# Queries of tiles 1 to 7 read from a second, transposed copy of the input and normalised on GpSimd in place of normalised rows transposed on TensorE

## The chip, the cores and the metric

The program runs on one core of one Trainium2 chip. Its engines are TensorE (PE, matmuls and transposes; its weight loads are shown apart as PEld), VectorE (DVE), ScalarE (ACT), GpSimd (POOL) and SyncE (SP, which here only issues transfers). Each engine takes its instructions in order; between engines there are semaphores. A transfer (DMA) is put on a queue by the engine that issues it, and an engine that has to wait before it issues one holds back everything behind it on that engine. The metric is device time in microseconds, the median of several executions; the profile is one further execution.

## The reference, cut to what matters

One layer in float32: cross-attention whose queries are the normalised input, then a gated MLP with a top-k selection, then a mixture of small experts. The change touches the first line alone.

```
def _layernorm(x, axis=-1, eps=1e-05):
    m = jnp.mean(x, axis=axis, keepdims=True)
    v = jnp.var(x, axis=axis, keepdims=True)
    return (x - m) / jnp.sqrt(v + eps)

def _L0_xattn_ref(q, k, v, start_pos, mask):       # 32 heads of 32, 8 key/value heads, 4 query heads each
    scores = jnp.einsum('bsgrd,btgd->bgrst', xq, xk) / math.sqrt(HEAD_DIM) + mask
    probs = jax.nn.softmax(scores, axis=-1)
    out = jnp.einsum('bgrst,btgd->bsgrd', probs, xv)

x = x + _L0_xattn_ref(_layernorm(x), ctx_1024, ctx_1024, 0, mask)   # x: 16 x 64 x 1024, ctx: 16 x 1601 x 256
x = x + _L0_attn_ref(_layernorm(x), w_gate, w_up, w_down)           # width 2752
x = x + _L0_ffn_ref(_layernorm(x), router_w, router_b, A, Bm)
```

## The kernel before, in words

The 16 x 64 = 1024 rows of x are cut into 8 tiles of 128 rows (NT = 8); tile i holds the batches 2i and 2i + 1. The first half of the program is the attention, the second the MLP and the experts, which a planner orders by costs; the change lies wholly in the first half, whose order on every engine is the order in which the Python program emits it (the helper `InOrder`, line 87, keeps it; as it emits every operation, all these instructions carry line 95 in the profile, so they are told apart by the names of their tiles).

The attention runs over 64 groups (lines 238 to 360): a group is one batch b, one half h of the 8 key/value heads, and one pair rh of the four query heads that share a key head. So a tile has 8 groups; in the loop at line 419, n is the group, m = n % 8 its place in the tile, and i = n // 8 + 1 is the *next* tile, whose queries are made ready in this one. Each turn of the loop has two halves, d = 0 and 1, and each half is one round of software pipelining:

- PE computes one half of the scores of the *next* group (`scores`, eight matmuls `ps` or `shared` <- kT, qt), then the value products of the *last* group (`values`, `shared` <- pT, v), then transposes the exponentials of two heads of *this* group (`turn`, 26 transposes `pt` <- ident, sc).
- DVE adds the mask and takes the maximum (`masked`, `sc` <- ps, mask), ACT takes the exponentials (`sc` <- sc, nm), and both copy the transposed blocks out of PSUM (`pT` <- pt).

The queries of tile i come about inside the turns of the tile before it. At m = 2 SP issues the load of x[i] (line 424). DVE takes the statistics of its two column halves at (m, d) = (4, 0) and (5, 0) (`Norm.half`). At (5, 1) DVE ends them, POOL raises the variance to the power -1/2 (`rstd_q`) and scales the rows (`scaled_rows`, `xn` <- x, mv_q, rstd_q, two instructions). At (6, 1) and (7, 1) `turn_queries` makes PE transpose four 128 x 128 blocks for each head half h (`ptq` <- ident, xn), and ACT copies them from PSUM to `qt` and multiplies by 1/sqrt(32). The scores of the first group of tile i, which read half h = 0 of `qt`, are emitted at (7, 0) of the turns before it, and half h = 1 is first read at m = 1 of its own turns. Tile 0 has its own path ahead of the loop.

Around this there are two streams of transfers. On SP's queue, `load_kv(b + 1)` (line 191) is emitted within `scores(0)` of the group (b, h = 0, rh = 1), that is at (m, d) = (4, 0) and (0, 0). It issues two key tiles (`kT`) and two value tiles (`v`, each in two transfers, 12 blocks and a tail of 65 rows). The pools `kT` and `v` have three buffers each, and a batch takes two of each, so the second key tile waits until the scores of (b, 0, 1) are done, and the second value tile until the *value products* of (b, 0, 1) are done: these are emitted two turns later, at m = 6 or m = 2, d = 1. On SP follow the x load at m = 2 and, at m = 4 before the keys, the store `xs` of a finished tile.

On POOL, `sums_in`, `sums_made` and `sums_out` (lines 166 to 180) prepare weight sums for the MLP, one unit a turn: a load of some 700 KB, four subtractions, a store. POOL also normalises and adds the attention's output (`finish_tile`, at (1, 1) and (2, 0): `att` <- att, rs and `x` <- x, att). The tile `att` and the tile `xn` take turns in one buffer (`xnp`, one buffer, tag xn).

```
        for d in range(2):
            ...
                following.scores(d)
            ...
                groups[n - 1].values(d)
            ...
            if i < NT and d == 1 and m >= 6:
                turn_queries(i, xn, m - 6)
            ...
            copies = group.turn((2 * d, 2 * d + 1))
            ...
                if (m, d) == (5, 1):
                    norm.end()
                    xn = scaled_rows(i, norm, pool)
```

Of the kernel before, what the change touches and what calls it, by code (L numbers as in the profile page):

```python
# [9 lines left out]
F32 = mybir.dt.float32  # L10
# [6 lines left out]
ALU = mybir.AluOpType  # L17
# [3 lines left out]
P = 128  # L21
B, S, D = 16, 64, 1024
T, C = 1601, 256
HD = 32
NT = B * S // P
# [26 lines left out]
EPS = 1e-5  # L52
# [4 lines left out]
def tile_perceiver_layer(  # L57
    ctx: ExitStack,
    tc: tile.TileContext,
    x_in: bass.AP,  # L60
    ctx_v: bass.AP,
    ctx_t: bass.AP,
    mask: bass.AP,
# [11 lines left out]
    dram = ctx.enter_context(  # L75
        tc.tile_pool(name="dram", bufs=1, space=bass.MemoryType.DRAM)
    )
    small = ctx.enter_context(tc.tile_pool(name="small", bufs=4))
# [3 lines left out]
    neg_half = const.tile([P, 1], F32, name="neg_half")  # L82
    nc.gpsimd.memset(neg_half, -0.5)

    x = {}

    class InOrder:


        def __init__(self, engine):  # L90
            self.engine = engine
# [7 lines left out]
    pe, dve, act = InOrder(nc.tensor), InOrder(nc.vector), InOrder(nc.scalar)  # L99
    pool, sp_queue = InOrder(nc.gpsimd), InOrder(nc.sync)  # L100

    class Norm:


        def __init__(self, xt, name):
            self.xt, self.name = xt, name
            self.st = small.tile([P, 2, 6], F32, tag="st", name=f"st_{name}")

        def half(self, j):
# [2 lines left out]
        def end(self):  # L112
            name = self.name
            mv = small.tile([P, 2], F32, tag="mv", name=f"mv_{name}")
            dve.bn_aggr(mv, self.st)
            ve = small.tile([P, 1], F32, tag="ve", name=f"ve_{name}")
            dve.tensor_scalar(ve, mv[:, 1:2], EPS, None, ALU.add)
            rstd = small.tile([P, 1], F32, tag="rstd", name=f"rstd_{name}")
            pool.tensor_tensor(rstd, ve, neg_half, ALU.pow)
            self.mean, self.rstd = mv[:, 0:1], rstd  # L120

# [5 lines left out]
    def new_pool(stack, name, bufs, side="left", space=bass.MemoryType.SB):  # L129
        return stack.enter_context(  # L130
            tc.tile_pool(name=name, bufs=bufs, side=side, space=space, reuse_waits="tile")
        )
# [3 lines left out]
    a1 = new_pool(early, "a1", 1)  # L136
    ktp = new_pool(early, "kT", 3)
    qtp = new_pool(early, "qT", 2)
    scp = new_pool(early, "sc", 2)
    xnp = new_pool(late, "xn", 1, "right")  # L140
# [30 lines left out]
    def sums_made(u):  # L171
        b11, b12, b21, b22 = (sums[u][:, j, :] for j in range(4))
        pool.tensor_tensor(b12, b12, b11, ALU.subtract)
        pool.tensor_tensor(b22, b22, b12, ALU.subtract)
        pool.tensor_tensor(b11, b22, b11, ALU.subtract)
        pool.tensor_tensor(b21, b21, b22, ALU.subtract)

    def sums_out(u):
        (_, t), _ = sum_columns(u)
        pool.dma_start(t, sums[u])  # L180

    def load_x(i, parts=1):
        x[i] = xp.tile([P, D], F32, tag="x", name=f"x{i}")
        for j in range(parts):
            cols = slice(j * D // parts, (j + 1) * D // parts)
            sp_queue.dma_start(x[i][:, cols], x_in[i * P : (i + 1) * P, cols])

    mask2 = a1.tile([P, T], F32, name="mask2")
    qT, kv, oT, rs_tok = {}, {}, {}, {}
# [25 lines left out]
    def scaled_rows(i, norm, engine):  # L215

        xn = xnp.tile([P, 2, 4, 4, HD], F32, tag="xn", name=f"xn{i}")
        xv = x[i].rearrange("p (h g r d) -> p h r g d", h=2, g=4, r=4)
        for h in range(2):
            engine.tensor_scalar(  # L220
                xn[:, h], xv[:, h], norm.mean, norm.rstd, ALU.subtract, ALU.mult
            )
        return xn

    def turn_queries(i, xn, h):

        if h == 0:
            qT[i] = qtp.tile([P, 2, 2, 4, S], F32, tag="qt", name=f"qt{i}")
        pt = ps_t.tile([P, 4, P], F32, tag="pt", name=f"ptq{i}_{h}")
        for r in range(4):  # L230
            pe.transpose(pt[:, r, :], xn[:, h, r].rearrange("p g d -> p (g d)"), ident)
        act.activation(
            qT[i][:, h].rearrange("p b r s -> p r b s"),
            pt.rearrange("p r (b s) -> p r b s", b=2),
            AF.Copy, scale=1.0 / math.sqrt(HD),
        )
# [127 lines left out]
    def finish_tile(i, h, home=ps_t, tag="pt"):  # L364


        if h == 0:
            att[i] = xnp.tile([P, 2, 4, 4, HD], F32, tag="xn", name=f"att{i}")
        rows = att[i][:, h]
        pt = home.tile([P, 4, P], F32, tag=tag, name=f"pto{i}_{h}")  # L370
        for r in range(4):
            pe.transpose(
                pt[:, r, :], oT[i][:, h, r].rearrange("p b s -> p (b s)"), ident
            )

        def add():
            pool.tensor_tensor(
                rows, rows, rs_tok[i][:, h].unsqueeze(3).to_broadcast([P, 4, 4, HD]),
                ALU.mult,
            )  # L380
            xv = x[i].rearrange("p (h g r d) -> p h r g d", h=2, g=4, r=4)
            pool.tensor_tensor(xv[:, h], xv[:, h], rows, ALU.add)

        return (rows, pt.rearrange("p r (g d) -> p r g d", g=4)), add
# [12 lines left out]
    norm = Norm(x[0], "q0")  # L397
# [3 lines left out]
    xn = scaled_rows(0, norm, dve)  # L401
# [17 lines left out]
    for n in range(ng):  # L419
        i, m = n // 8 + 1, n % 8  # L420
        group = groups[n]
        last = n == ng - 1
        if m == 2 and i < NT:
            load_x(i)
        if m == 4 and n > 8:
            sp_queue.dma_start(xs[i - 2], x[i - 2])
        if n == ng - 3:
            for j in range(2):
                x[j] = xp.tile([P, D], F32, tag="x", name=f"x{j}_f")
                sp_queue.dma_start(x[j], xs[j])  # L430
        for d in range(2):
            add = None
            following = groups[n + 1] if not last else None
            if following:
                following.scores(d)
            if n > 0:
                groups[n - 1].values(d)
            if following:
                following.masked(d)
            on_act = [0, 1, 2] if last else [0, 1, 2, 3, 5]  # L440
            if i < NT and d == 1 and m >= 6:
                turn_queries(i, xn, m - 6)
            if n > 8 and 3 <= 2 * m + d <= 4:
                copy, add = finish_tile(i - 2, 1 - d)
                act.copy(*copy)
            copies = group.turn((2 * d, 2 * d + 1))
            for j, copy in enumerate(copies):
                if j in on_act:
                    act.copy(*copy)
                else:  # L450
                    dve.tensor_copy(*copy)
            if n > 0:
                groups[n - 1].keep(d)
                if d == 1:
                    groups[n - 1].inverse()
            for g in range(2):
                if d == 0:
                    group.softmax(2 + g)
                elif following:
                    following.softmax(g)  # L460
            if add:
                add()
            if i < NT:
                if (m, d) == (4, 0):
                    norm = Norm(x[i], f"q{i}")
                if (m, d) in ((4, 0), (5, 0)):
                    norm.half(m - 4)
                if (m, d) == (5, 1):
                    norm.end()
                    xn = scaled_rows(i, norm, pool)  # L470
            if d == 1 and 0 <= n - 3 < 3 * NU:
                sums_made(n - 3)
                sums_out(n - 3)
            if d == 1 and 0 <= n - 2 < 3 * NU:
                sums_in(n - 2)
            if last:
                xn = first[d].tile([P, D], F32, tag=("xn", "oT")[d], name=f"xn_f{d}")
                norm = Norm(x[d], f"f{d}")
                norm.half(0)
                norm.half(1)  # L480
                norm.end()
                dve.tensor_scalar(xn, x[d], norm.mean, norm.rstd, ALU.subtract, ALU.mult)
                first_xn[d] = xn
# [49 lines left out]
    s, hS, held_h, hs, a, marked = {}, {}, {}, {}, {}, {0: [], 1: []}  # L533
# [716 lines left out]
    over = add("PE", 1.1, end, [t] + hs[0], rank["g0"] - 5)  # L1250
# [36 lines left out]
class Plan:  # L1287
# [20 lines left out]
    def add(self, engine, cost, emit, deps, rank, takes=None, frees=None, margin=0.0):  # L1308
        holds, frees = (
            [hold for hold in (h if isinstance(h, tuple) else (h,)) if hold]  # L1310
            for h in (takes, frees)
        )
        task = self.Task(engine, cost, emit, deps, rank, holds, margin)
        for hold in frees:
            hold.freed_by = task
        self.tasks.append(task)
        return task
# [98 lines left out]
```

## Time and profile before

| | |
|---|---|
| median of 3 executions | 1696.45 us (1695.98 to 1696.63) |
| the profiled execution | 1695.55 us, of which its span (first to last instruction) is 1693.7 us |
| busy share of the span | PE 98%, DVE 85%, ACT 75%, POOL 33% |
| attention | from the start to about 818 us |
| granted TensorE clock, mean | 0.996 of full speed |
| transfers | 384.53 MB, mean 227 GB/s |

In lists of instructions the fields are: start, time taken, engine, line, operation, the tile written <- the tiles read, shapes, count; an idle time in square brackets is what the engine waited before it and for whom. In groups and tiles, three numbers with strokes are the shortest, the middle and the longest duration in ns. In lists of transfers the last number is the middle time in us from the issue to the landing.

### The profile page before, as it was taken

How to read it: one execution, taken by the hardware profiler on the slowest of the kernel's cores; microseconds unless marked ns; L12 is line 12 of the kernel's file. 1: busy time of each engine (PE TensorE's matmuls, PEld its weight loads, DVE VectorE, ACT ScalarE, POOL GpSimd, SP SyncE). 2: the span in 40 equal slices, each digit the busy share in tenths (PEclk: the TensorE clock that was granted, in tenths of full speed). 3: DMA queues.
4: the chain of work that ended last, by engine and by line, in shares of the span. 5: the costliest groups of instructions: out<-in, count | busy, mean ns of one | idle time of the engine just before them, and what ended most of it. 6: DMA issues, size and time to landing. Idle time of an engine off the chain costs nothing. (4 is left out here: it accounts for less than half of the span.)

```text
span 1693.7 us, 38371 instructions
## 1 busy us (share of the span) xinstructions
PE 1666.9 (98%) x15098; PEld 1190.4 (70%) x15098; DVE 1437.5 (85%) x3654; ACT 1262.8 (75%) x1716; POOL 560.1 (33%) x584
## 2 busy tenths in 40 slices
PE   8999999999999999999899999999989999999998
PEld 6888888888888888888666666645645646645644
DVE  7998989899898988988429999999999999999603
ACT  6999999999999999999246675677467772778010
POOL 2045455455545544110121212222381023430631
PEclk9999999999999999999999999999989999999999
DMA  8245656565564655131799999988959979888973
GB/s 252 92 131 185 209 165 213 180 220 167 196 216 153 221 192 190 41 97 61 275 293 330 306 291 307 290 277 274 345 175 302 307 248 320 273 297 270 324 262 135
DMA packets 132018, 384.53 MB, mean 227 GB/s; under 512 B 9440, under 2 KB 60928, under 8 KB 131840
## 3 DMA queue, kind: packets, MB, share of 16 engines
q1 hardware_dynamic: 112976, 312.83, 56.2%
q0 software_dynamic: 18432, 68.16, 11.6%
q8 instruction: 120, 1.97, 0.5%
q10 hardware_dynamic: 432, 1.09, 0.2%
q14 instruction: 58, 0.48, 0.1%
HBM read 339.58 MB, written 42.47 MB: 226 GB/s over the span
## 5 line engine op out<-in xcount | busy, mean ns | idle before, releaser
L95 DVE CUSTOM_DVE_ANT_0 sc<-ps,mask 128x512 f32<-128x512 f32 (+2 forms) x896 | 468.3, 587 | 30.4 <-PE ps L95 29.1
L95 ACT ACTIVATE sign<-a,cand 128x2752 int8<-128x2752 f32 x136 | 351.8, 2587 | 111.0 <-DVE cand L95 111.0
L95 ACT ACTIVATE sc<-sc,nm 128x1601 f32<-128x1601 f32 x256 | 415.7, 1629 | 9.3 <-DVE nm L95 9.3
L95 PE MATMUL pt<-ident,sc 128*128 128x128 f32 (+1 forms) x3328 | 390.5, 274 | 1.9 <-ACT sc L95 1.7
L95 DVE TENSOR_SCALAR_CACHE_REDUCE junk<-a,cand 128x2752 uint8<-128x2752 f32 x124 | 381.7, 3078 | 4.0
L95 PEld LDWEIGHTS pt<-ident,sc 128*128 128x128 f32 (+1 forms) x3328 | 362.0, 141 | 22.9 <-issue 19.0
L95 ACT COPY pT<-pt 128x512 f32<-128x512 f32 x636 | 335.5, 599 | 23.4 <-PE pt L95 11.9
L95 POOL TENSOR_TENSOR tw<-tw 128x344 f32<-128x344 f32 (+1 forms) x192 | 176.0, 927 | 275.9 <-DMA tw<-in_wg_dram 93.0
L95 PE MATMUL pg_g<-w_g,hS 128*128 128x344 f32 x896 | 262.9, 455 | 2.8 <-DMA w_g<-ts 2.1
L95 PE MATMUL pg_u<-w_u,hS 128*128 128x344 f32 x896 | 263.4, 452 | 0.0
L95 PEld LDWEIGHTS pg_g<-w_g,hS 128*128 128x128 f32 x896 | 170.6, 191 | 91.8 <-issue 4.9
L95 PE MATMUL pd<-w_d,s 128*128 128x512 f32 x528 | 233.9, 597 | 0.0
L95 PEld LDWEIGHTS pg_u<-w_u,hS 128*128 128x128 f32 x896 | 169.0, 190 | 87.2 <-issue 3.1
L95 PE MATMUL shared<-pT,v 128*32 128x128 f32 x6656 | 208.1, 274 | 3.6 <-DVE oT L95 3.6
L95 PE MATMUL ps<-kT,qt 32*128 32x512 f32 (+2 forms) x1792 | 210.9, 538 | 0.3 <-DVE mx L95 0.3
L95 PEld LDWEIGHTS shared<-pT,v 128*32 128x32 f32 x6656 | 174.1, 110 | 52.1 <-issue 45.1
L95 PEld LDWEIGHTS pd<-w_d,s 128*128 128x128 f32 x528 | 99.3, 192 | 114.8 <-issue 113.4
L95 DVE COPY pT<-pt 128x512 f32<-128x512 f32 (+1 forms) x260 | 139.9, 558 | 45.2 <-PE pt L95 45.2
L95 PEld LDWEIGHTS ps<-kT,qt 32*128 32x128 f32 x1792 | 97.7, 184 | 52.8 <-DVE pT L95 27.5
L95 ACT ACTIVATE s<-s 128x344 f32<-128x344 f32 (+1 forms) x70 | 36.5, 535 | 75.8 <-DVE s L95 75.7
L95 POOL TENSOR_TENSOR s<-s,rank 128x688 f32<-128x688 f32 x32 | 62.4, 1963 | 77.5 <-DVE rank L95 76.9
L95 DVE DVE_READ_ACCUMULATOR2_ANT mx<- 128x1 f32 x1024 | 84.3, 82 | 0.0
(326 smaller groups left out, 1411.7 us busy)
## 6 DMA issues: line engine op xcount, KB each, us to landing
w_g<-ts SPq DMA_DIRECT2D x64, 688.0 KB, 4.2
w_u<-ts SPq DMA_DIRECT2D x64, 688.0 KB, 4.2
w_d<-ts SPq DMA_DIRECT2D x48, 768.0 KB, 4.2
w_g<-in_wg_dram SPq DMA_DIRECT2D x48, 688.0 KB, 4.1
w_u<-in_wu_dram SPq DMA_DIRECT2D x48, 688.0 KB, 4.8
w_d<-in_wd_dram SPq DMA_DIRECT2D x36, 768.0 KB, 5.1
kT<-in_ctx_t_dram SPq DMA_DIRECT2D x31, 800.5 KB, 6.7
v<-in_ctx_v_dram SPq DMA_DIRECT2D x32, 768.0 KB, 5.3
```

What stands on the lines that cost most here:

```text
L95: return tc.keep_in_program_order(getattr(self.engine, op)(*args, **kwargs))
```

## The change

A second copy of x, `x_q`, is laid out on the host: for each tile 128 partitions (four key heads by 32 head dimensions) by 1024 columns (h, batch, r, row). A tile of it is what the transposes made, without the normalisation. As mean and 1/std belong to the columns of that copy, they have to lie along the free axis and on every partition: they are written to device memory (256 floats) and read back to all partitions (`row`, 128 x 256). POOL then subtracts and multiplies, four instructions of 128 x 512. The factor 1/sqrt(32) goes into the variance, which is multiplied by 32 before the power.

In order: at (4, 0) the statistics begin and SP is given the load of `xq`, into the buffer of `xn`; at (4, 1) they end, POOL takes the power, and SP is given the store of `stats` and the load of `row`; at (5, 1) POOL is given the four instructions that write `qt`. The transposes at (6, 1) and (7, 1) and ACT's copies of them are gone. `load_kv` of (4, 0) is emitted ahead of all three new transfers, as it is part of `scores(0)`.

```
         def end(self):
...
-            dve.tensor_scalar(ve, mv[:, 1:2], EPS, None, ALU.add)
-            rstd = small.tile([P, 1], F32, tag="rstd", name=f"rstd_{name}")
-            pool.tensor_tensor(rstd, ve, neg_half, ALU.pow)
-            self.mean, self.rstd = mv[:, 0:1], rstd
+            dve.tensor_scalar(ve, mv[:, 1:2], EPS, self.over, ALU.add, ALU.mult)
+            pool.tensor_tensor(mv[:, 1:2], ve, neg_half, ALU.pow)
+            self.mean, self.rstd, self.both = mv[:, 0:1], mv[:, 1:2], mv
...
+    def row_tile(i):
+        row = a1.tile([P, 2, P // S, S], F32, tag="row", name=f"row{i}")
+        stats = dram.tile([1, 2 * P], F32, tag=f"stats{i}", name=f"stats{i}")
+        sp_queue.dma_start(
+            stats.rearrange("o (k p) -> (o p) k", k=2), norm.both
+        )
+        sp_queue.dma_start(
+            row.rearrange("p k b s -> p (k b s)"), stats.to_broadcast([P, 2 * P])
+        )
+        return row
+
+    def load_queries(i):
+        raw = xnp.tile([P, 2, 4, 4, HD], F32, tag="xn", name=f"xq{i}")
+        raw = raw.rearrange("p h r g d -> p (h r g d)")
+        sp_queue.dma_start(raw, x_q[i])
+        return raw.rearrange("p (h b r s) -> p h b r s", h=2, b=P // S, r=4)
+
+    def scale_queries(i, raw, row):
+        qT[i] = qtp.tile([P, 2, 2, 4, S], F32, tag="qt", name=f"qt{i}")
+        mean, rstd = (
+            row[:, k].unsqueeze(2).to_broadcast([P, P // S, 4, S]) for k in range(2)
+        )
+        for h in range(2):
+            pool.tensor_tensor(raw[:, h], raw[:, h], mean, ALU.subtract)
+            pool.tensor_tensor(qT[i][:, h], raw[:, h], rstd, ALU.mult)
...
-            if i < NT and d == 1 and m >= 6:
-                turn_queries(i, xn, m - 6)
...
                 if (m, d) == (4, 0):
-                    norm = Norm(x[i], f"q{i}")
-                if (m, d) in ((4, 0), (5, 0)):
-                    norm.half(m - 4)
+                    norm, raw = Norm(x[i], f"q{i}", float(HD)), load_queries(i)
+                if m == 4:
+                    norm.half(d)
+                if (m, d) == (4, 1):
+                    norm.end()
+                    row = row_tile(i)
                 if (m, d) == (5, 1):
-                    norm.end()
-                    xn = scaled_rows(i, norm, pool)
+                    scale_queries(i, raw, row)
```

More of the change, by code (lines that the diff above doesn't have):

```diff
@@ L60, in tile_perceiver_layer @@
     x_in: bass.AP,
+    x_q: bass.AP,
     ctx_v: bass.AP,
@@ L102, in tile_perceiver_layer, with __init__ @@
     class Norm:
-        def __init__(self, xt, name):
-            self.xt, self.name = xt, name
+        def __init__(self, xt, name, over=1.0):
+            self.xt, self.name, self.over = xt, name, over
             self.st = small.tile([P, 2, 6], F32, tag="st", name=f"st_{name}")
@@ L1389, in wide @@
         return w.transpose(3, 0, 5, 1, 4, 2).reshape(4, P, GW)
+    x_q = np.asarray(x).reshape(NT, P // S, S, 2, 4, 4, HD)
+    x_q = x_q.transpose(0, 4, 6, 3, 1, 5, 2).reshape(NT, P, D)
     laid_out = {
         "x": np.asarray(x).reshape(B * S, D),
+        "x_q": x_q,
         "ctx_v": ctx_v,
```

## The prediction

> **What bounds the kernel now.** I read the page's engine shares first, then the order of PE around the place where the queries are used, then SP's own waits, then POOL, and last the landing times of transfers. The first lines are the page's shares and its slices for PE.
>
> ```profile
> PE 1666.9 (98%) x15098; PEld 1190.4 (70%) x15098; DVE 1437.5 (85%) x3654; ACT 1262.8 (75%) x1716; POOL 560.1 (33%) x584
> ...
> PE   8999999999999999999899999999989999999998
> ```
>
> In the attention (the left half) PE has no idle slice: whatever makes PE wait there lengthens the run one for one, and whatever PE loses shortens it. The timeline of PE at the end of tile 2's turns, where tile 3's queries are due, shows where each half ends:
>
> ```profile
> 294.60 1.38 PE L95 MATMUL ps<-kT,qt 32*128 32x512 f32 x11
> ...
> 296.16 1.74 PE L95 MATMUL shared<-pT,v 128*32 128x128 f32 x56
> 297.83 0.66 PE L95 MATMUL ptq<-ident,xn 128*128 128x128 f32 x4
> 298.32 3.00 PE L95 MATMUL pt<-ident,sc 128*128 128x128 f32 x26
> 301.25 1.38 PE L95 MATMUL ps<-kT,qt 32*128 32x512 f32 x11
> ```
>
> The first four lines are (m, d) = (6, 1): scores, value products to 297.9, the query transposes of h = 0, the 26 transposes. At 301.25 the half (7, 0) begins with the first scores of tile 3; they are the first to read the new `qt`. The next half has no slack before it: there is no bracket with an idle time.
>
> SP's waits in total, SP's timeline over the same stretch, and one later place on SP:
>
> ```profile
> SPq L95 <- PE shared L95: 642.0, 44, 24.1
> ```
>
> ```profile
> 297.96 1.16 SPq L95 DMA_DIRECT2D v<-in_ctx_v_dram  x2
> 299.16 0.36 SPq L95 DMA_DIRECT2D kT<-in_ctx_t_dram  x1
> ```
>
> ```profile
> 747.44 0.35 SPq L95 DMA_DIRECT2D xs<-x  x1
> 747.88 5.56 SPq L95 DMA_DIRECT2D x_f<-xs  x2
> ```
>
> This decides the case. SP stands for 642 us behind the value products: the second `v` load of a batch needs the buffer that they free. The one emitted at (4, 0) is released at 297.96, right after the products of (6, 1). What is emitted behind it in SP's order (here the next batch's kT) starts at 299.16, 1.20 us later. In the other six tiles the pair stands the same way (v at 99.14, 198.54, 397.37, 496.78, 596.19, 695.60, each 3.3 us ahead of the scores that open the next tile). Landing times:
>
> ```profile
> v<-in_ctx_v_dram SPq DMA_DIRECT2D x32, 768.0 KB, 5.3
> ...
> out_dram<-s SPq DMA_DIRECT2D x16, 256.0 KB, 2.4
> x<-in_x_dram SPq DMA_DIRECT2D x7, 512.0 KB, 5.8
> ...
> x_f<-xs SPq DMA_DIRECT2D x2, 512.0 KB, 3.2
> ```
>
> **What goes.** For each of 7 tiles, 8 query transposes: `ptq` starts at 297.83 and the next work at 298.32, so 0.49 us of PE for a half h, 0.98 us a tile, 6.9 us in all. They lie on the bound, so the gain is real. Also gone: ACT's 14 copies to `qt` at 0.60 us (8.4 us), and POOL's 14 `xn` instructions at 2.07 us (29 us). Both engines keep up with PE here (PE waited for ACT's `sc` 1.7 us in the whole run), so these count nothing.
>
> **What moves.** `xq`, `stats` and `row` are issued by SP, in program order. `load_kv` of (4, 0) is emitted ahead of them within `scores(0)`, so all three stand behind the second `v` load, and that waits until the value products of (6, 1) end. They are emitted at (4, 0) and (4, 1), about 30 us ahead of use, but can start only at the place of the 299.16 line. The first scores of the next tile come, with the `ptq` of (6, 1) gone, 301.25 - 0.49 - 297.96 = 2.80 us after the `v` issue. I call that issue t0 and add up:
>
> - `xq` is issued at t0 + 1.20. Its 512 KB stand behind 768 KB of `v`. The nearest row is the 747.44 store: also 512 KB, also 1.26 us behind a `v` load (746.18), and the next `x_f` needs its end: that one is issued at 753.1, 5.7 us after the store. The x load, likewise behind a `v`, took 5.8 us. From below: not before `v` itself, whose shortest landing is 5.0 us (t0 + 5.0). From above: x at 6.0 us (t0 + 7.2). I take 5.7, t0 + 6.9.
> - `stats`, 256 runs of 4 bytes to device memory, is issued at t0 + 1.55 on the same queue. No row shows such a store. From below it lands with `xq` (0 more). From above it takes a whole 5.7 us more, as the loaded store. The smallest store shown is `out`, 2.4 us alone; its fixed part overlaps the end of `xq`, so I take half, 1.2 us: t0 + 8.1.
> - `row`, 128 KB read back, can be issued only when `stats` has landed. From above `x_f`, 3.2 us; from below that less its 512 KB at the 0.4 MB/us at which the transfers run when busy, 1.9 us. Between them and nearer to a small transfer, 2.4 us: t0 + 10.5.
> - POOL: subtract and multiply of h = 0, at 1.07 us (`att` <- att, rs, 128x512 with a broadcast) and 0.08 us between: 2.2 us, with a hand-over 2.3. From above 1.29 each (`x` <- x, att), 2.8. `qt` h = 0 is ready at t0 + 12.8. h = 1, 2.3 us later, is read only at m = 1: no cost.
>
> So PE waits 12.8 - 2.8 = 10.0 us in each of 7 tiles: 70 us. Bounds: 5.0 + 0 + 1.9 + 2.2 - 2.8 = 6.3 us and 7.2 + 5.7 + 3.2 + 2.8 - 2.8 = 16.1 us.
>
> The Trainium skill ("DMA: Bandwidth & Descriptors", Anatomy of one DMA and Rules for kernel authors) puts a fixed cost of about 2.0 us on a transfer, most of it the receipt from the target memory, and says that a strided last dimension costs one descriptor per element; it is a rule against this store. By it alone `stats` and `row` one after the other would be some 4.0 us where my rows gave 3.6, an estimate that would add 3 us over seven tiles.
>
> **The clock after a wait.** The run has one long gap in dense PE work, at 835, where PE waited 2.05 us for `w_g`:
>
> ```profile
> 834.00:835.00 1.00, 1.00 (x4) 0.38 (x2) 0.00 (x0) 0.00 (x0) 0.00 (x0) 1.00 0.99 405
> ...
> 837.00:838.00 1.00, 0.86 (x2) 0.64 (x3) 0.00 (x0) 0.00 (x0) 0.00 (x0) 0.70 1.03 429
> 838.00:839.00 1.00, 1.00 (x3) 0.60 (x2) 0.00 (x0) 0.00 (x0) 0.00 (x0) 0.50 1.04 429
> 839.00:840.00 1.00, 1.00 (x3) 0.53 (x3) 0.00 (x0) 0.00 (x0) 0.00 (x0) 0.50 0.99 413
> 840.00:841.00 1.00, 1.00 (x4) 0.63 (x3) 0.00 (x0) 0.00 (x0) 0.00 (x0) 0.59 1.02 424
> ```
>
> The field before the DMA share is the granted clock: 0.30 + 0.50 + 0.50 + 0.41 = 1.7 us lost after PE had resumed, that is 3.4 us at half clock. A gap of 10 us is five times as long, so I charge 1.7 us a tile, 11.9 us. From below nothing (the run's first transposes, at 1.35 us, have 1.00); from above two such stretches, 3.4 us.
>
> The Trainium skill ("TensorE: Matmul & The Clock Gate", Part 1) has the same half clock and a window of about 3.4 us, but says that it takes an idle gap of a whole window; here 2.05 us was enough, so the row stands. For 10 us the page charges the same 1.7 us or, with a second window, 3.4.
>
> **What is hidden, and by what.** The power on POOL comes before `stats`. It stands ahead of the sums unit that ran at 285.23, 13 us before t0. If that cover went, `stats` would be later by what is missing. Behind the waiting `scale_queries` on POOL stand the sums units, whose cycle is 11.4 us (subtractions at 261.53 and 272.99), paced by their own loads. After the wait POOL has 8 units: a first without a wait (5.6 us) and seven at 11.4, and is back at the next `scale_queries` some 100 us after t0; the next data are ready after a period of 110 and 10.5 more, so 20 us are left. It would take units of over 14 us for POOL to add to the wait. `att` and `xs` come later by up to a group; the key loads behind `xs` are used four turns later. The kT of the next batch goes out some 7 us later on SP; its scores come two turns or more later. The extra DVE multiply sits in an instruction that is there anyway.
>
> The sum: 7 x (10.0 + 1.7) - 6.9 = +75 us. Against the profiled execution's 1695.55 that is 1770.6; it stands 0.9 below the median, so for the median 1771.5. Bounds: 7 x 6.3 - 6.9 = +37 (1733.6) and 7 x (16.1 + 3.4) - 6.9 = +130 (1826).
>
> **The rivals.**
> - *A short chain*: `stats` lands with or ahead of `xq`, as both are on the queue together and POOL is silent meanwhile, and the clock is not cut. For it: the v-load's stretch is shared with POOL's transfers today, and will not be. Against: 768 + 512 KB at 0.4 MB/us are 3.2 us of pure traffic. It gives waits of 6.3 to 7.5 us with 0 to 1 for the clock: 1734 to 1749.
> - *A slow store*: the 4-byte runs take as long as a big store. For it: no row shows them. It gives waits of 13 to 16.1 us with 2.5 to 3.4 for the clock, 1798 to 1826.
> - *Not slower*: PE does not wait, and the 6.9 us of transposes are won, 1689.5. That takes one thing: that the second `v` load of (4, 0) is released before (6, 1). The chain is 12.8 us and PE's lead 2.8, so the release would have to come 10 us, nearly two halves, earlier for no wait at all, and 9 us earlier to break even. Against it: seven times out of seven the release comes at the products of (6, 1), and the change does not touch those buffers.
> - *POOL becomes the bound*, through units of over 14 us: each us more costs 8 us a tile in the later tiles. At 15 us a unit it would be some 50 us more, 1820. Against: the loads of the sums get quieter company.
>
> **How the numbers follow.** Forecast (waits of 7.5 to 13 us, clock 1 to 2.5): 72 in 100, its own range 1749 to 1798. Short chain 12, slow store 10, POOL the bound 2, not slower 4. The range for 8 in 10 takes half of the short chain and half of the slow store: 1741 to 1808. This kernel's measurement cannot tell less than 0.2% (3.4 us) from no change; the faster side is the third rival, 3 in 100, and 1 in 100 is left for a tie; slower has 96.
>
> **What the profile will show.** Right: PE idle some 10 us before `ps` in seven places about 110 us apart, released by POOL's `qt`; `xq` issued 1.2 us after the second `v`; SP waiting for the landing of `stats`; half clock after each gap; no `ptq` but tile 0's. Wrong: `xq` issued at (4, 0) well ahead of the value products, PE's gaps under 5 us, or gaps that grow from tile to tile (POOL late). Wrong also if PE's halves lengthen elsewhere.

## The result, and the profile after

The changed kernel takes 1828.05 us (median of 5, 1827.17 to 1830.17); the kernel before, 1695.98 us (median of 5, 1691.44 to 1696.63). The ratio is 1.0788, with a 95% interval from 1.0772 to 1.0804: 132 us slower. The forecast had 75 us and a range that ended at 1808, so the direction and the place were right and the size was not.

First the page of the changed kernel: engine shares, and the slices of PE, of ACT and of the granted clock.

```profile
PE 1680.9 (92%) x15042; PEld 1192.2 (65%) x15042; DVE 1438.3 (79%) x3654; ACT 1257.7 (69%) x1702; POOL 563.8 (31%) x598
...
PE   9969979699696996987989999999989999999998
...
ACT  5959959599596895986974467667747774677210
PEclk8979989899898997998999999999999999999999
```

A slice is 45.6 us. PE's row, which had no hole in the attention, now has one every two to three slices, ACT has it with PE, and the clock is low in the same slices. The right half is as it was. PE's waits and SP's waits, in total, times and longest:

```profile
PE ps L96 <- POOL qt L96: 118.9, 7, 17.3
```

```profile
SPq L96 <- PE shared L96: 679.4, 44, 29.9
...
SPq L96 <- DMA stats<-mv_q: 69.1, 7, 10.2
```

Seven waits of 17 us on the mean, one for each tile, and SP stood 69.1 us waiting for `stats` to land. The third tile's chain, on SP, on POOL and on PE:

```profile
338.82 1.12 SPq L96 DMA_DIRECT2D v<-in_ctx_v_dram  x2
339.99 0.35 SPq L96 DMA_DIRECT2D xq<-in_x_q_dram  x1
340.44 0.37 SPq L96 DMA_DIRECT2D stats<-mv_q  x1
350.79 0.34 SPq L96 DMA_DIRECT2D row<-stats  x1
351.18 0.42 SPq L96 DMA_DIRECT2D kT<-in_ctx_t_dram  x1
```

```profile
355.72 1.26 POOL L96 TENSOR_TENSOR xq<-xq,row 128x512 f32<-128x512 f32 x1 [24.46 <-DMA row<-stats]
357.06 1.26 POOL L96 TENSOR_TENSOR qt<-xq,row 128x512 f32<-128x512 f32 x1
```

```profile
338.69 3.06 PE L96 MATMUL pt<-ident,sc 128*128 128x128 f32 x26
358.37 2.56 PE L96 MATMUL ps<-kT,qt 32*128 32x512 f32 x11 [16.62 <-POOL qt L96]
```

With t0 = 338.82, as in the prediction, `xq` goes out at t0 + 1.17, where the forecast had 1.20; `row` goes out at t0 + 12.0, where the forecast had 8.1; POOL starts at 16.9, not 10.5; PE resumes at 19.6, not 12.8. The same stretch in windows of 2 us (busy time of PE, PEld, DVE, ACT, POOL; then granted clock, DMA share, GB/s):

```profile
346.00:348.00 2.00, 0.00 (x0) 0.00 (x0) 0.00 (x0) 0.00 (x0) 0.00 (x0) 0.72 0.00 0
348.00:350.00 2.00, 0.00 (x0) 0.00 (x0) 0.00 (x0) 0.00 (x0) 0.00 (x0) 0.50 0.00 0
...
362.00:364.00 2.00, 2.00 (x42) 1.58 (x32) 2.00 (x9) 0.00 (x0) 1.92 (x3) 0.51 0.00 0
364.00:366.00 2.00, 2.00 (x22) 1.96 (x19) 0.61 (x4) 1.21 (x3) 1.70 (x3) 1.00 0.04 8
```

From 346 to 350 nothing at all works: every engine is idle and no bytes move, and yet `stats` has not landed. The clock is at half from about 347 until 364, so PE runs for 5.6 us at half clock after it has resumed at 358.37. What moved just before, in two stretches (344.50 to 345.25, then 345.25 to 350.80):

```profile
DMA packets 305, 0.07 MB, mean 94 GB/s; under 512 B 288, under 2 KB 288, under 8 KB 305
```

```profile
DMA packets 0, 0.00 MB, mean 0 GB/s; under 512 B 0, under 2 KB 0, under 8 KB 0
```

The small packets, those of `stats` among them, stand together with the last large ones of `xq`, some 4.3 us after the store was issued; the trace has the end of `xq`'s bytes at 345.13. `row` goes out only 5.7 us later, with not one packet from 345.25 on. In the seven tiles it is 4.4 to 6.0 us from the end of `xq`'s bytes to the issue of `row`, 5.5 on the mean.

Setting the starts of the 128 halves of the attention beside those of before gives where the time went, in us over the run:

| | sum | per tile |
|---|---|---|
| PE's waits for `qt` | +118.9 | 17.0 |
| first half-turn after each wait, longer than the 5.99 us of before (half clock) | +15.2 | 2.2 (1.4 to 2.9) |
| the two halves without query transposes | -6.1 | 2 x 0.44 |
| the half that now ends the statistics | +2.7 | 0.38 |
| the first half-turn of the run | +2.9 | once |
| the rest of the program | -2.1 | |
| difference of the two spans, 1825.2 - 1693.7 | +131.5 | |

The first half-turn's share is not put down to the change: the profile has a stretch of half clock there, from 15.8 to 26.0 us, and so has the kernel before with a store added (18.2 to 25.0), while two variants of the changed kernel that are the same so early have none.

### The profile page after: what moved, and what is told of

The parts are those of the page before. It is cut to its first block, busy times and chain, and to the rows that moved or that the text cites. A ratio compares the mean times of both kernels' runs of the same rounds, so it can differ in the third digit from the quotient of the medians.

```text
span 1825.2 us, 38286 instructions
## 1 busy us (share of the span) xinstructions
PE 1680.9 (92%) x15042; PEld 1192.2 (65%) x15042; DVE 1438.3 (79%) x3654; ACT 1257.7 (69%) x1702; POOL 563.8 (31%) x598
## 3 DMA queue, kind: packets, MB, share of 16 engines
q0 software_dynamic: 18432, 68.16, 11.5%
## 5 line engine op out<-in xcount | busy, mean ns | idle before, releaser
L96 PE MATMUL pt<-ident,sc 128*128 128x128 f32 (+1 forms) x3328 | 396.6, 276 | 1.2 <-ACT sc L96 0.8
L96 PE MATMUL ps<-kT,qt 32*128 32x512 f32 (+2 forms) x1792 | 221.7, 563 | 119.8 <-POOL qt L96 118.9
L96 PEld LDWEIGHTS ps<-kT,qt 32*128 32x128 f32 x1792 | 102.0, 191 | 178.6 <-POOL qt L96 120.6
L96 PE MATMUL shared<-pT,v 128*32 128x128 f32 x6656 | 213.0, 279 | 3.6 <-DVE oT L96 3.6
L96 PEld LDWEIGHTS shared<-pT,v 128*32 128x32 f32 x6656 | 177.8, 112 | 55.4 <-issue 48.5
L96 PE MATMUL shared<-kT,qt 32*128 32x289 f32 (+1 forms) x256 | 86.9, 419 | 0.0
```

Source lines behind the costliest of these rows:

```text
L96: return tc.keep_in_program_order(getattr(self.engine, op)(*args, **kwargs))
```

## Experiments

The first question was whether the place on SP makes the wait (my theory), or whether store, read-back and four POOL instructions are too slow a chain wherever they stand (the rival). Two kernels move them away from the second `v` load in different ways.

**All three transfers ahead of `load_kv`.**

```
+        if m == 4 and i < NT:          # at the top of the turn, before scores(0) and its load_kv
+            raw = load_queries(i)
+            row = row_tile(i)
...
-                if (m, d) == (4, 0):  ... load_queries(i)
-                if m == 4: norm.half(d)
-                if (m, d) == (4, 1): norm.end(); row = row_tile(i)
+                if (m, d) == (3, 1):
+                    norm = Norm(x[i], f"q{i}", float(HD)); norm.half(0); norm.half(1); norm.end()
```

> The changed kernel, but both halves of the statistics and the power are taken at (3, 1), and SP is given xq, stats and row at m = 4 ahead of load_kv, so none of the three stands behind a v load. Theory (the order on SP): row lands some 30 us before the first scores that read qt, PE's wait for POOL's qt (118.9 us in 7 places) falls to nothing, the half clock after it too, and what stays is the 6.9 us of transposes won: 1689 us, 0.4% under the kernel before. Rival (the chain of store, read-back and POOL's four instructions is too long or POOL is too late, wherever it is issued): waits of 5 us or more stay and the time is above 1730.

**A fourth `v` buffer.**

```
-    vp = new_pool(late, "v", 3, "right")
+    vp = new_pool(late, "v", 4, "right")
```

> The changed kernel with four v buffers in place of three and nothing else: the second v load of (4, 0) no longer waits for the value products of (6, 1); SP is then held at most by the second kT load, which the scores of (4, 1) release, some 25 us before the new tile's first scores. Theory: the three new transfers start there, are done 18 us later, and PE's seven waits go: 1689 to 1695 us. Rival (the chain itself, or POOL): as now, about 1828.

Measured: 1716.76 us (ratio 1.0158, 1.0117 to 1.0199) and 1717.36 us (1.0127, 1.0112 to 1.0142). The fourth buffer alone, with nothing else touched, takes away 111 of the 132 us, and PE's waits for `qt` fall from 118.9 us in 7 places to 19.9 in 3; in the first variant to 6.2 in 1. So the place behind the `v` load is the main cause. But neither kernel came down to 1689: some 28 us were in neither account, and the expectation was wrong there.

What is left in the fourth-buffer kernel begins on POOL. In tile 5, which has the longest wait, on POOL and on SP:

```profile
489.35 3.89 POOL L96 TENSOR_TENSOR tw<-tw 128x352 f32<-128x352 f32 x4 [10.59 <-DMA tw<-in_wd_dram]
...
495.08 0.58 POOL L96 TENSOR_TENSOR mv_q<-ve_q,neg_half 128x1 f32<-128x1 f32 x1
```

```profile
495.68 0.37 SPq L96 DMA_DIRECT2D stats<-mv_q  x1
506.31 0.34 SPq L96 DMA_DIRECT2D row<-stats  x1
```

The power stands on POOL behind a sums unit that waited for its load, and `stats` goes out 0.03 us after the power ends, so that the chain starts too late. It is so in all three tiles with a wait. The prediction had named this cover: if it went, `stats` would be later by what is missing.

The first variant shows another part. Around its first store of `stats`, on SP, in windows (columns as above), and on PE:

```profile
69.63 0.38 SPq L96 DMA_DIRECT2D stats<-mv_q  x1
81.17 0.33 SPq L96 DMA_DIRECT2D row<-stats  x1
```

```profile
72.00:74.00 2.00, 2.00 (x20) 1.60 (x21) 2.00 (x9) 1.63 (x4) 1.69 (x3) 1.00 0.00 0
74.00:76.00 2.00, 2.00 (x59) 1.60 (x57) 1.69 (x6) 2.00 (x3) 1.23 (x2) 1.00 0.49 188
76.00:78.00 2.00, 0.97 (x23) 0.53 (x12) 2.00 (x10) 0.88 (x2) 0.00 (x0) 1.00 2.47 82
78.00:80.00 2.00, 0.00 (x0) 0.00 (x0) 0.00 (x0) 0.00 (x0) 0.00 (x0) 1.00 0.24 12
80.00:82.00 2.00, 1.96 (x11) 1.86 (x12) 0.45 (x2) 0.29 (x1) 0.00 (x0) 0.64 0.61 175
```

```profile
80.04 2.18 PE L96 MATMUL pt<-ident,sc 128*128 128x128 f32 x11 [3.07 <-issue]
```

It is 11.5 us here from the store's issue to that of `row`, although nothing stands ahead of it: no bytes moved in the windows from 70 to 74 but its own. Its packets are on record between 70.5 and 70.8, 1.0 us after the issue, so 10.4 us passed after the last of them. POOL had issued a 688 KB store and a 688 KB load at 73.7 and 74.5; they get through for about 2 us, then moving falls to 12 GB/s until `stats` is through at 81. And PE stands for 3.07 us with "issue": it waited for nothing that the profile shows. This led to a second theory: the store of 256 four-byte runs is not only slow, it holds up others.

**Without the store**, in the changed kernel and in the first variant. `row` is read from the second copy of x, so both leave out the true mean and 1/std and do otherwise the same work.

```
-        stats = dram.tile([1, 2 * P], F32, ...)
-        sp_queue.dma_start(stats.rearrange("o (k p) -> (o p) k", k=2), norm.both)
-        sp_queue.dma_start(row..., stats.to_broadcast([P, 2 * P]))
+        sp_queue.dma_start(row..., x_q[i][0:1, : 2 * P].to_broadcast([P, 2 * P]))
```

> The changed kernel without the store of stats: row is filled from 1 KB of the second copy of x (so the queries are scaled with wrong numbers; the work on every engine is the same), at the same place on SP. The store held SP for 10.3 us before row could go. Theory, with the store as the term that was sized too small: row goes out 1.6 us after the v load in place of 12.0, lands together with xq at about 8 us, POOL needs 2.6, PE waits 8 us a tile in place of 17, and the clock still costs 2 to 3: 7 x 11 less 6.9 us over the kernel before, about 1765 us. Rival (the read-back and what stands on the queue make the wait, the store is hidden by xq): above 1800.

> The kernel of e1_ahead_of_kv (1716.8 us) without the store of stats; row is filled from 1 KB of the second copy of x (wrong scale, same work). In e1 PE had gaps of up to 3.1 us that end with 'issue', and one wait of 6.2 us for POOL, while after each store the DMA engines moved under 30 GB/s for 4 to 6 us and POOL's sums loads took 10 us to land in place of 7. Theory (the store of 256 four-byte runs holds up everything else on the DMA engines, also what feeds PE and POOL): both go, 7 x (1.0 for the statistics in one half less 0.9 for the transposes) is left, about 1697 us, and the sums loads land in 7 us. Rival (the gaps come from xq and the key loads ahead, or POOL is too slow anyway): 1710 us or more.

Measured: 1764.61 us (1.0411, 1.0396 to 1.0427), where about 1765 was expected, with seven waits of 7.3 to 8.7 us; and 1695.72 us (1.0009, 0.9998 to 1.0021), with no wait for `qt` and none of the first variant's gaps that end with "issue". The store is worth 63 us behind the `v` load and still 21 us where it is issued ahead of it. In the second kernel the remainder is what was worked out: the half with all the statistics is 0.97 us longer, the two without transposes are 0.44 shorter each.

**The store alone**, added to the kernel before, read by nobody:

```
                 if (m, d) == (5, 1):
                     norm.end()
+                    stats = dram.tile([1, 2 * P], F32, tag=f"stats{i}", name=f"stats{i}")
+                    sp_queue.dma_start(stats.rearrange("o (k p) -> (o p) k", k=2), norm.both)
```

> The kernel before, with the store of stats added behind the second v load, which nothing waits for or reads. Theory (the store holds up other transfers by itself): PE gets gaps that end with 'issue', and POOL's sums load beside the store lands some 4 us later; 1 to 4 us a tile, 1703 to 1720 us. Rival (a store that nobody waits for costs nothing): 1696 us, within 0.2%.

Measured: 1715.26 us (1.0114, 1.0096 to 1.0131): seven stores of 1 KB that nobody waits for cost 20 us. The first one, on SP and on POOL; below it the same load of POOL in the kernel before:

```profile
102.79 0.39 SPq L95 DMA_DIRECT2D stats<-mv_q  x1
```

```profile
103.58 0.76 POOL L95 DMA_DIRECT2D tw<-in_wg_dram  x1
121.07 3.82 POOL L95 TENSOR_TENSOR tw<-tw 128x344 f32<-128x344 f32 x4 [16.73 <-DMA tw<-in_wg_dram]
```

```profile
101.16 0.76 POOL L95 DMA_DIRECT2D tw<-in_wg_dram  x1
112.04 3.79 POOL L95 TENSOR_TENSOR tw<-tw 128x344 f32<-128x344 f32 x4 [10.13 <-DMA tw<-in_wg_dram]
```

The load that POOL issued 0.8 us after the store came in 17.5 us later; in the kernel before, the load in the same place, beside the same `v` load, took 10.9 us (the middle one of all such loads 6.9). In the profile PE gets gaps of up to 1.3 us that end with "issue", and once, in tile 6, waits 5.2 us for POOL's `xn`. That is the rival of POOL as the bound, in small: POOL does become late, not through its own work but through its loads. In the fourth-buffer kernel the sums loads ahead of the two longest waits took over 11 us as well, but no store of `stats` stands beside those, and the kernel before has six loads of 10 to 12 us too: that these came late is not shown to be the store's doing.

**Half as many runs**, of 8 bytes:

```
-        row = a1.tile([P, 2, P // S, S], F32, ...)
+        row = a1.tile([P, P // S, S, 2], F32, ...)
...
-            stats.rearrange("o (k p) -> (o p) k", k=2), norm.both
+            stats.rearrange("o (p k) -> (o p) k", k=2), norm.both
...
-            row[:, k].unsqueeze(2).to_broadcast([P, P // S, 4, S]) for k in range(2)
+            row[:, :, :, k].unsqueeze(2).to_broadcast([P, P // S, 4, S]) for k in range(2)
```

> The changed kernel with stats stored as 128 runs of 8 bytes in place of 256 of 4 (mean and 1/std side by side, read by POOL with a step of two). If the landing of the store (10.3 us from its issue to row's) goes by the number of runs, the part beyond xq's own landing is halved: row 2 to 4 us earlier, 14 to 28 us in all, 1800 to 1814. If it is a fixed cost of a store of small pieces: 1828.

Measured: 1801.17 us (1.0627, 1.0613 to 1.0641). From the issue of `stats` to that of `row` it is 6.3 us on the mean of the seven tiles, after 10.3: 4.0 us less for half the runs and the same bytes. From the last bytes of `xq` to `row` it is 1.8 us, after 5.5. So the form of the runs sets the time and not the 1 KB; as each run is also twice as long, number and length of the runs are not told apart. The third tile, on SP:

```profile
331.59 0.37 SPq L96 DMA_DIRECT2D stats<-mv_q  x1
337.36 0.33 SPq L96 DMA_DIRECT2D row<-stats  x1
```

**What else stands on the queue.** One kernel loads `xq` alone ahead of `load_kv`; another puts a small store behind `row` that waits for POOL's `qt`, and so keeps the 800 KB of the next `kT` off the DMA engines while `row` is read.

```
+        if m == 4 and i < NT:
+            raw = load_queries(i)        # stats and row stay at (4, 1)
```

> The changed kernel with the load of xq alone moved ahead of load_kv at m = 4; stats and row stay behind the second v load. The prediction let the store land 1.2 us after xq because both stand on one queue. If xq was part of the wait (the store starts when xq is through), the store lands about 1 to 2 us earlier after the v load's 768 KB, and the time is 1814 to 1822. If the store needs its 10 us from its own issue whatever stands ahead of it, it is issued 0.45 us earlier and that is all: 7 x 0.45 = 3 us less, 1825. Should the wait go away altogether, the place of xq was the cause and not stats.

```
                     scale_queries(i, raw, row)
+                    held = dram.tile([1, S], F32, tag=f"held{i}", name=f"held{i}")
+                    sp_queue.dma_start(held, qT[i][0:1, 0, 0, 0, :])
```

> The changed kernel with one store of 256 bytes of qt added on SP behind row: it waits for POOL's qt, so the next kT load (800 KB), which goes out 0.4 us after row in the changed kernel, starts only when the chain is over. If row's 4.9 us from issue to POOL's start come from sharing the DMA engines with kT, row lands in 2 to 3 us, PE's waits are 2 to 3 us shorter, and the time is 1807 to 1815. If row needs that by itself (128 reads of the same 1 KB), 1828.

Measured: 1815.85 us (1.0716, 1.0692 to 1.0739) and 1822.73 us (1.0750, 1.0726 to 1.0774). The first lies in the range that was expected if `xq` was part of the wait (1814 to 1822), yet the part is small: with `xq` away the store is issued 0.3 us earlier on the mean and takes 9.5 us in place of 10.3, and the wait is 1.3 us a tile shorter. The store's packets now stand some 3.2 us after its issue, behind `v` alone, and 5.4 us pass after the last of them, as in the changed kernel. The second lies between its two expectations, nearer to the one in which `row` needs the time by itself: without `kT` beside it, `row` needs 4.6 us from its issue to POOL's start, after 5.2, so sharing is a small part too. Of these 4.6 us some 2.0 pass before its first packet. Why 128 reads of one and the same 1 KB need so long is not settled; reading 128 different rows was not tried.

**PE kept busy through the wait.**

```
+            if (m, d) == (7, 0) and following:
+                fill = ps_t.tile([P, 4, P], F32, tag="pt", name=f"fill{n}")
+                for _ in range(130):
+                    pe.transpose(fill[:, 0, :], ident, ident)
```

> The changed kernel with 130 transposes of the identity (about 15 us) added on PE ahead of the first scores of each turn (7, 0), that is in the wait. Theory (after each wait PE runs at half clock for 5.6 us, which costs 2.8 us a tile, and the engines need no time to fill again): the wait stays by the clock of the chain but the clock stays full, 7 x 2.8 = 20 us less, about 1808 us. Rival (what the wait costs beyond its length is the pipeline filling again): 1828 or more.

Measured: 1822.87 us (1.0748, 1.0727 to 1.0768), 5 us less, not 20. The fill ended before the queries were there, and PE still stood 2.7 to 5.5 us; in five of seven tiles half clock followed (after 2.73, 3.16, 3.37, 4.55 and 5.52 us). In the other two (2.80 and 3.26 us) it did not, and they answer the question. Here is one, on PE; the next half begins at 242.91:

```profile
219.76 14.36 PE L96 MATMUL fill<-ident 128*128 128x128 f32 x130
236.92 1.38 PE L96 MATMUL ps<-kT,qt 32*128 32x512 f32 x11 [2.80 <-POOL qt L96]
242.91 1.38 PE L96 MATMUL ps<-kT,qt 32*128 32x512 f32 x11
```

With the clock at 1.00 the first half after the wait takes 5.99 us, exactly as in the kernel before; in the tiles with half clock it takes 1.4 to 2.9 us more. So the engines need no time to fill again, and what a wait costs beyond its length is the clock. That this is worth 2.2 us a tile stands; that a fill gives it back was true in part only: the clock fell in five tiles all the same, and the chain itself was 0.8 us longer with the fill.

**Without a transfer for `row`.** `xq` goes ahead of `load_kv`, and PE makes `row`:

```
+                if (m, d) == (4, 1):                      # statistics at (3, 1) and (4, 0)
+                    norm.end()
+                    for k in range(2):
+                        pool.tensor_scalar(diag[:, k], ident, norm.both[:, k : k + 1], None, ALU.mult)
+            if i < NT and (m, d) == (5, 1):               # in row_tile, ahead of the turn's transposes
+                pe.matmul(pt, ones, diag, start=True, stop=True)    # 128x256: every row is mean, 1/std
+                act.copy(row, pt)
```

> xq is loaded ahead of load_kv at m = 4, and row takes no transfer at all: POOL multiplies the identity by mean and by 1/std (two 128x128), PE multiplies that by ones (one matmul, 256 columns), ACT copies 128x256 to SBUF; the statistics are spread over (3, 1), (4, 0), (4, 1). Theory: no waits; PE gives back 0.98 us a tile and pays 0.2: 7 x 0.75 = 5 us under the kernel before, 1691 us. Rival (POOL, with four instructions of 1.26 us and two small ones, cannot deliver in time at a period of 99 us): waits for POOL's qt of some us in several tiles, 1700 to 1720.

Measured: 1691.87 us against 1694.94 for the kernel before in the same runs (median of 12), ratio 0.9981, from 0.9972 to 0.9991. It is the one variant that beats the kernel before: by 3.1 us, or 0.2%. POOL in tile 3 (PE's first scores of the new tile come at 302.26):

```profile
279.61 1.19 POOL L96 TENSOR_SCALAR diag<-ident,mv_q 128x128 f32<-128x128 f32 x2
...
291.12 1.29 POOL L96 TENSOR_TENSOR xq<-xq,row 128x512 f32<-128x512 f32 x1
292.49 1.29 POOL L96 TENSOR_TENSOR qt<-xq,row 128x512 f32<-128x512 f32 x1
```

No wait for POOL's `qt` is left. Each tile wins 2 x 0.44 us and pays 0.48 in the half with the matmul: 0.4 us, or 2.8 in all. The rival of a POOL that cannot deliver at a period of 99 us falls with it: here POOL has the first half of `qt` ready 4.5 to 11.8 us ahead of its use.

## Why the forecast was right in kind and wrong in size

- *What bounds*: PE, in the attention, without slack. Right: 118.9 us of waits are 118.9 us of time.
- *The place*: `xq`, `stats` and `row` behind the second `v` load, released at the products of (6, 1). Right in all seven tiles; the fourth buffer shows it by taking that one wait away. Only the 642 us that were read as SP's wait behind value products were not all that: in the kernel before, some 350 us are waits of `v` loads, and some 280 are waits of second `kT` loads, which scores release.
- *What goes*: 0.98 us a tile was too much. Two halves shorter by 0.44 are 0.88, and the statistics, which the forecast let move for nothing, make the half at (4, 1) 0.38 us longer: DVE had less room there than was assumed. With all of them in one half it was 0.97.
- *`xq` at t0 + 6.9, `stats` 1.2 us after it*: the first part was nearly right, as `xq`'s last bytes are on record at t0 + 6.5 on the mean. The second part is the step that failed most. I let the end of `xq` hide the store, and took half of the smallest store on the page, 2.4 us for 256 KB. The store's packets did go out with the end of `xq`, but `row` could be issued only 5.5 us after that, in place of 1.2: at t0 + 12.0 in place of 8.1, 3.9 us a tile. From its issue the store needs about 10 us wherever it stands: 10.3 behind `xq`, 9.5 without it, 10.5 on the mean in the first variant. The row to look at was not the smallest store in bytes, and none with many short runs was in the trace: the same 1 KB in 128 runs of 8 bytes takes 6.3. The page of the Trainium skill that the forecast weighed, "DMA: Bandwidth & Descriptors", Anatomy of one DMA, has about 2.0 us for a transfer's fixed cost, fitted to transfers that GpSimd issues; the runs show that such a store, issued by SP, is far from it.
- *`row` 2.4 us*: 5.2 us measured, beyond the upper end of 3.2 that was taken from a 512 KB load. This is the second term that failed, 2.8 us a tile, of which sharing with `kT` is 0.6.
- *POOL 2.3 us*: 2.65; the four instructions take 1.26 us each, as the strided `x` <- x, att (1.29), not as `att` <- att, rs (1.07). PE came 0.1 us later. Together: 10.0 + 3.9 + 2.8 + 0.4 - 0.1 = 17.0.
- *The clock 1.7 us*: 2.2 us, and it is the clock and nothing else. Right in kind, within its bounds. The lower bound of nothing rested on a misreading: the clock records of the kernel before begin only at 4.55 us, and its first transposes take 421 ns each until then and 273 ns after.
- *The bounds*: of the wait, 6.3 to 16.1 us, measured 17.0. It was `row` that went past them; the store's 5.5 us after `xq` lie within its own, 0 to 5.7. The "slow store" rival, with just these 5.7 us, came nearest and had 10 in 100; it should have had more, as an operation that no row shows at all was priced by rows of another kind, and at the low side.
- *POOL has 20 us to spare*: right in the changed kernel, where POOL stands idle for 21 to 37 us before it scales the queries. In the kernels without the wait the room is smaller, and it was used up in the fourth-buffer kernel, where the power came late on POOL.
- *What was not seen*: that the store costs others something, 20 us with nobody waiting for it. In the changed kernel no load of POOL stands beside the store (no packet from 345.25 to 350.80 in the third tile; no sums load takes over 10 us in the run), so it does not show as an extra.

What stays open: why the store takes 5 us and more after its last packet, and by what it holds up other transfers and PE. Late instruction loads, which are transfers too, would be an idea for PE's gaps with "issue", but the trace does not bear it out: around the first variant's gap that ends at 80.04 us the instruction transfers on record are at 65.4 and at 81.4 us, the second one after PE had resumed.

## What to carry to other kernels

Before a transfer is added, find what is queued ahead of it on its engine and what that waits for: here three transfers that were written two turns early could start only when PE was 2 us from needing them, because the load ahead of them waited for a `v` buffer. A transfer of many short runs is not to be priced by its bytes, nor by rows of large transfers, and what it does to the transfers beside it belongs to its price. Where a few numbers have to reach all partitions, a diagonal and a matmul with ones cost PE 0.5 us a tile and POOL 1.2 us; a store and a read-back took 15 us.

## What the runs showed of the hardware that was not expected

- A store of 256 runs of 4 bytes from 128 partitions to device memory took 10.3 us from its issue to that of the read-back that waited for it, 128 runs of 8 bytes 6.3 us; for 5.5 us of the 10.3 no bytes moved. A load that POOL issued beside one came in after 17.5 us, not 10.9, and with seven such stores the whole program became 20 us longer.
- After a wait of 17 us TensorE ran at half clock for 3 to 6 us more. The length of a wait alone did not decide this: half clock followed waits of 2.05 us in the kernel before and of 2.73 and 3.16 us after a fill of identity transposes, and did not follow waits of 2.80 and 3.26 us after the same fill.
